# Attention of a conditioned transformer block: lasting PSUM tiles, a split first exp, repeated q and k transfers

## The chip, the cores and the metric

The kernel runs on one core of one Trainium2 chip. The metric is the device time of one execution in microseconds. The kernel before took 3331.09 us (median of 3 runs, 3324.33 to 3333.92).

The core has a matrix engine (TensorE, "PE" in the profile, its weight loads "PEld"), a vector engine (DVE), a scalar engine for functions such as exp (ACT), GpSimd (POOL) and a queue engine (SP) that issues most of the transfers ("SPq"). The engines run their own instruction streams in order and wait for each other by semaphores. TensorE writes its sums to PSUM, which has eight banks of 128 partitions x 512 fp32 values.

## The reference

One block with adaptive layer norm (adaLN) over x of shape 2 x 2048 x 576, with 16 heads of 36 features. The part that matters here is the attention; the rest is cut:

```python
xn = _ln(x, 1e-06)
xn = xn * (1 + sc_msa[:, None, :]) + sh_msa[:, None, :]
qkv = (xn @ w_qkv + b_qkv).reshape(B, N, 3, H, hd)
q, k, v = (qkv[:, :, 0], qkv[:, :, 1], qkv[:, :, 2])
q = _ln(q, 1e-05, qn_g, qn_b)
k = _ln(k, 1e-05, kn_g, kn_b)
attn = jnp.einsum('bqhd,bkhd->bhqk', q, k) * scale
attn = jax.nn.softmax(attn, axis=-1)
o = jnp.einsum('bhqk,bkhd->bqhd', attn, v).reshape(B, N, C)
o = o @ w_proj + b_proj
x = x + g_msa[:, None, :] * o
...
h = jax.nn.gelu(xn2 @ w1 + b1, approximate=False)
m = h @ w2 + b2
x = x + g_mlp[:, None, :] * m
```

Everything is fp32. The kernel has two branches; with these inputs the one called `block_of_small` runs, whose exp needs no maximum.

## The kernel before

**Stages.** For each of the two batches: the qkv projection and head norms (`inputs`), the attention (`attend`), and the output projection (`outputs`). Then the two products of the MLP for both batches. In the trace the attention of the first batch is the stretch from 268 to 1082 us, that of the second from 1396 to 2198 us.

**How q and k lie.** A head has 36 features. 32 of them go to the rows of a "main" tile (`km`, `qm`), one head to each group of 32 partitions, so that four score products run side by side in four row groups. The last four features go to an "ends" tile (`ke`, `qe`) as four parts in 16 rows: each of the four values stands there four times, and `parted` (L767, L768) makes the high or low part of each on DVE with a mask by row (`low_k`, `low_q`). `rows_taken` issues the transfers that fill these tiles out of the projected features (`qo`, `kr`), all on SP's queue: L755 the main rows, L758 the ends, one transfer for each of the four copies. `take_q` does so for one block of 512 queries, `take_k` for all keys of one pair of heads, `take_k_block` for some token tiles of the first pair's keys. Each returns the `parted` work, to be done later.

**The loop of groups.** `attend` goes over 8 head pairs x 4 query blocks x 4 groups, 128 groups in a batch. A group takes four tiles of 128 keys, two at a time (`scores`, L974): each of the four score tiles, called A, B, C, D below in their order, has two halves of 512 queries, one for each head, and each half is a bank of its own. A and B are written together by eight products, then C and D. An exp (L979, ACT) turns a score tile into a `pt` tile in SBUF; there are five `pt` buffers. `values` (L988) then sums the products of v with the four `pt` tiles into the first half of a further PSUM tile, called the sum here. DVE takes the sum out to `ot`: L1034 copies it in the first group of a block, L1036 adds it in the others. TensorE runs one group ahead: its order is scores of group n+1, values of group n, scores of group n+2, and so on. TensorE's and DVE's order in the attention is that of the code; ACT, POOL and SP follow the order that the building layer gives them.

**PSUM.** All PSUM tiles of the attention come from `s_tile`, a pool of four buffers of two banks, which is all of PSUM. A group takes five in turn: A, B, C, D and the sum. So the sum that is made after the scores of a group gets the buffer of that group's A, and the next group's D gets the buffer of that sum. A product into a new tile waits for the last user of the buffer.

**What is put in between.** `later` is a list of work to do some groups later: the masks of `take_q` two groups on, of `take_k` four, the end of a block three (`finish` writes the row sums to DRAM and reads them back over 64 partitions, L1003 and L1004; then `divided` takes the reciprocal, L1007, multiplies, L1008, and issues the stores into `qo`, L1013). `ot` has two buffers, so the copy of L1034 waits for those stores of two blocks ago. `hooks` puts other work into single groups: the transposes of the last two token tiles of q and k (L874, `last_inputs`) in the first four groups, the adaLN products of the first batch in three later ones, and the transfers of the output weights. A hook's own PSUM tile comes from `s_tile` too.

Of the kernel before, what the change touches and what calls it, by code (L numbers as in the profile page):

```python
# [16 lines left out]
P = 128  # L17
# [14 lines left out]
def dit_block(  # L32
# [40 lines left out]

    const = ctx.enter_context(tc.tile_pool(name="const", bufs=1))
    dram = ctx.enter_context(tc.tile_pool(name="dram", bufs=1, space=bass.MemoryType.DRAM))
    psum = {}

    @contextmanager
    def psum_pools():
# [4 lines left out]
            yield  # L84

    def s_tile():
        return psum["s"].tile([P, 2, 512], F32, tag="s", name="s")

    def acc_tile():
# [616 lines left out]
    def block_of_small():  # L706
# [25 lines left out]
        high = kv.tile([P, BLK], F32R, name="high")  # L732

        low_k, low_q, sign_k, sign_q = (kv.tile([P, 1], F32, name=f"part{i}") for i in range(4))
        eights = ident.rearrange("p (r a b) -> p r a b", r=4, a=4)[:, :, 1, :]
        fours = ident.rearrange("p (r a b d) -> p r a b d", r=4, a=4, b=2)[:, :, 0:2, 1, :]
        nc.vector.tensor_reduce(low_k, eights, AX.XY, ALU.add)
        nc.vector.tensor_reduce(low_q, fours, AX.XYZ, ALU.add)
        for low, sign in ((low_k, sign_k), (low_q, sign_q)):
            nc.vector.tensor_scalar(sign, low, -2.0, 1.0, ALU.mult, ALU.add)  # L740
        nc.gpsimd.memset(vv[:, :, :, HD : HD + 1], 1.0)
# [3 lines left out]
        def chunk(c, cols):  # L745
            return qo[:, c, cols] if c < NKC else kr[:, c - NKC, cols]


        def rows_taken(main, ends, halves, first, src, dst):

            for c in halves:
                for h in range(2):
                    r0 = 32 * (2 * c + h)
                    for i, row, d, n in head_rows(first + h * HD, DIMS):
                        nc.sync.dma_start(out=main[r0 + d : r0 + d + n, dst], in_=chunk(i, src(c))[row : row + n, :])  # L755
                    ((i, row, _, n),) = head_rows(first + h * HD + DIMS, HD - DIMS)
                    for j in range(4):
                        nc.sync.dma_start(  # L758
                            out=ends[r0 + n * j : r0 + n * j + n, dst], in_=chunk(i, src(c))[row : row + n, :]
                        )  # L760

        def parted(ends, rows, low, sign):

# [8 lines left out]
        def take_k(p):  # L772
            m, e = km[p % 2], ke[p % 2]
            src = lambda c: slice(c * N // 2, (c + 1) * N // 2)
            rows_taken(m, e, range(2), C + p * 2 * HD, src, slice(0, N // 2))
            return lambda: parted(e, slice(0, P), low_k, sign_k)

        def take_k_block(t0, t1):

            c, k0 = divmod(t0 * P, N // 2)  # L780
            dst = slice(k0, k0 + (t1 - t0) * P)
            rows_taken(km[0], ke[0], (c,), C, lambda c: slice(t0 * P, t1 * P), dst)
            return lambda: parted(ke[0][:, dst], slice(64 * c, 64 * c + 64), low_k, sign_k)

        def take_q(p, qb):
            i = qb % 2
            src = lambda c: slice(qb * BLK, (qb + 1) * BLK)
            rows_taken(qm[i], qe[i], range(2), p * 2 * HD, src, slice(0, BLK))
            return lambda: parted(qe[i], slice(0, P), low_q, sign_q)

        def last_chunk(dst, w, groups, f):
# [162 lines left out]
        def attend(b, pool, hooks):  # L954

            def scores(p, qb, g):  # L960
                i, j = p % 2, qb % 2
                pts = []
                for k0 in (2 * g * P, (2 * g + 1) * P):
                    keys = slice(k0, k0 + P)
                    tiles = [s_tile() for c in range(2)]
                    for k, q, first in (
                        (km[i], qm[j], True),
                        (ke[i].bitcast(F32R), qe[j].bitcast(F32R), False),
                    ):
                        for c in range(2):  # L970
                            for h in range(2):
                                r0 = 32 * (2 * c + h)
                                r = slice(r0, r0 + (DIMS if first else 4 * (HD - DIMS)))
                                nc.tensor.matmul(  # L974
                                    tiles[c][:, h, :], k[r, keys], q[r, :], start=first, stop=not first
                                )
                    for c, ps in enumerate(tiles):
                        pt = pool.tile([P, 2, BLK], F32, name="pt", bufs=5)
                        nc.scalar.activation(pt, ps, AF.Exp, scale=SCALE)  # L979
                        pts.append((pt, k0 // P + c * NT // 2))  # L980
                return pts

            def values(p, pts):
                acc = s_tile()[:, 0, :]
                for pt, kc in pts:
                    for h in range(2):
                        v0 = (kc * H + 2 * p + h) * HV
                        nc.tensor.matmul(  # L988
                            acc[64 * h : 64 * h + 64, :],
                            vt[:, v0 : v0 + 64],  # L990
                            pt[:, h, :],
                            start=pt is pts[0][0],
                            stop=pt is pts[-1][0],
                        )
                return acc

            def finish(p, qb, ot):


                den = pool.tile([P, BLK], F32, name="den")  # L1000
                for h in range(2):
                    sums = den_dram[b, p, qb, h, :]
                    nc.sync.dma_start(out=sums.unsqueeze(0), in_=ot[64 * h + HD : 64 * h + HD + 1, :])  # L1003
                    nc.sync.dma_start(out=den[64 * h : 64 * h + 64, :], in_=sums.partition_broadcast(64))  # L1004

                def divided():
                    nc.vector.reciprocal(den, den)  # L1007
                    nc.vector.tensor_tensor(ot, ot, den, ALU.mult)  # L1008
                    cols = slice(qb * BLK, (qb + 1) * BLK)
                    for h in range(2):  # L1010
                        for c, row, d, n in head_rows((2 * p + h) * HD):
                            for r in (row,) if c < FULL else (row, row + 64):
                                nc.sync.dma_start(  # L1013
                                    out=qo[r : r + n, c, cols], in_=ot[64 * h + d : 64 * h + d + n, :]
                                )

                return divided

            steps = [(p, qb, g) for p in range(NPAIR) for qb in range(NBLK) for g in range(NG)]


            behind, later = None, [[] for _ in range(5)]
            for p, qb, g in [*steps, (None, None, None)]:
                pts = None if p is None else scores(p, qb, g)
                if g == 0 and (p, qb) != (NPAIR - 1, NBLK - 1):
                    later[2].append(take_q(*((p, qb + 1) if qb + 1 < NBLK else (p + 1, 0))))
                if g == 1 and qb == 1 and p + 1 < NPAIR:
                    later[4].append(take_k(p + 1))
                if behind is not None:
                    bp, bqb, bg, bpts = behind  # L1030
                    acc = values(bp, bpts)
                    if bg == 0:
                        ot = pool.tile([P, BLK], F32, name="ot", bufs=2)
                        nc.vector.tensor_copy(ot, acc)  # L1034
                    else:
                        nc.vector.tensor_tensor(ot, acc, ot, ALU.add)  # L1036
                    if bg == NG - 1:
                        later[3].append(finish(bp, bqb, ot))
                if (p, qb, g) in hooks:
                    later[1] += hooks[p, qb, g]() or []  # L1040
                later.append([])
                for do in later.pop(0):
                    do()
                behind = (p, qb, g, pts)
            for do in [do for group in later for do in group]:
                do()
# [80 lines left out]
        for b in range(B):  # L1127
# [30 lines left out]
            def output_opened():  # L1158
# [2 lines left out]
            hooks = {  # L1161
                (0, 0, 0): lambda: last_inputs(NT - 2, range(NKC - 1, NQK)),
                (0, 0, 1): lambda: last_inputs(NT - 1, range(NKC - 1, NQK)),
                (0, 0, 2): lambda: last_inputs(NT - 2, range(NKC - 1)),
                (0, 0, 3): last_inputs_done,
                (4, 0, 1): output_opened,
            }
            if b == 0:
                hooks |= {
                    (0, 2, 1): ada_opened,  # L1170
                    (1, 0, 2): ada_gates,
                    (2, 0, 2): ada_feature_rows,
                    (2, 0, 3): ada_features,
                }
            with tc.manual_schedule(engines={mybir.EngineType.DVE}):
                attend(b, att, hooks)
            close_att()
            wp, close_wp = opening["wp"]
            if b + 1 < B:
# [352 lines left out]
```

## Time and profile before

| What | us |
|---|---|
| Median of 3 runs | 3331.09 |
| The profiled execution's own time | 3329.74 |
| Its span, first to last instruction | 3327.5 |
| TensorE busy | 3250.7 |
| DVE busy | 1457.9 |
| ACT busy | 1440.7 |
| POOL busy | 255.0 |
| TensorE busy in 268.0 to 1082.2 (attention, first batch) | 798.26 of 814.20 |
| ACT busy there | 498.31 |
| TensorE busy in 1390.0 to 2197.6 (attention, second batch) | 794.48 of 807.60 |
| ACT busy there | 503.11 |

The granted clock of TensorE was 0.994 over the span. A line of the page's list of groups names the line of the kernel, the engine, the operation, what is written and read, and the count, then busy time and the mean of one. A line of the timeline begins with the start and the length in us; in brackets stands the idle time of the engine before it and who ended it. A busy TensorE isn't a TensorE at its peak: its instructions overlap, and an instruction that is held at the front of its queue can stand beside one that still runs.

### The profile page before, as it was taken

Reading aid. Unit: us, or ns where it says so; the run is one execution under the profiler, and the core shown is the slowest. Engines: PE = TensorE matmul, PEld = TensorE weight load, DVE = VectorE, ACT = ScalarE, POOL = GpSimd, SP = SyncE. Lnnn points to the kernel's source line nnn. Section 1 sums busy time; section 2 is a strip of 40 time slices with the busy share of each in tenths; the row PEclk is TensorE's granted clock in tenths of the full one; section 3 lists DMA queues with packets and bytes.
Section 4 is the critical chain, followed back from the end, with each engine's and each line's share of the span. In section 5 each row is a group of like instructions: output and inputs, shape, how many; then the busy total and the mean of one; then the engine's idle time right before and its main releaser. Section 6 shows DMA issues by size and latency. Waiting matters only on the chain.

```text
span 3327.5 us, 47009 instructions
## 1 busy us (share of the span) xinstructions
PE 3250.7 (98%) x18143; PEld 1892.2 (57%) x18143; DVE 1457.9 (44%) x2073; ACT 1440.7 (43%) x1928; POOL 255.0 (8%) x249
## 2 busy tenths in 40 slices
PE   8999999999999999999999999998999999999998
PEld 5774333333333777633333333357888788777776
DVE  4664333333333366533333333255455443554554
ACT  2335656666666033356666666633555543000000
POOL 1110000000000211100000000041000000111111
PEclk9999999999999999999999999999999999999999
DMA  3002212212111401021111111144322222523321
GB/s 127 26 27 62 73 44 64 54 45 52 45 44 29 143 26 30 18 57 44 42 42 43 36 44 41 35 169 145 120 84 88 81 81 77 191 100 119 130 100 37
DMA packets 123324, 234.28 MB, mean 70 GB/s; under 512 B 22412, under 2 KB 65365, under 8 KB 121045
## 3 DMA queue, kind: packets, MB, share of 16 engines
q1 hardware_dynamic: 112124, 193.10, 18.8%
q0 software_dynamic: 10240, 36.61, 3.2%
q8 instruction: 146, 2.39, 0.3%
q10 hardware_dynamic: 728, 1.48, 0.1%
q14 instruction: 86, 0.70, 0.1%
HBM read 125.96 MB, written 56.91 MB: 55 GB/s over the span
## 4 chain that ended last, share of the span: by engine, by line
PE 86%; ACT 7%; issue 2%; DMA 2%; DVE 1%; SPq 1%; POOL 0%; ACTq 0%; DVEq 0%; POOLq 0%
PE s L988 28%; PE s L1460 14%; PE s L360 14%; PE s L974 11%; PE m L1310 11%; ACT pt L979 7%; PE m L1324 2%; PE s L371 2%; PE one L1310 2%; PE s L874 1%; DMA wb<-in_w_dram 1%; PE t L1369 1%; SPq L758 0%; PE s L338 0%; DMA qo<-ot 0%
## 5 line engine op out<-in xcount | busy, mean ns | idle before, releaser
L979 ACT ACTIVATE pt<-s 128x1024 f32<-128x1024 f32 x1024 | 994.1, 1024 | 611.2 <-PE s L988 348.0
L988 PE MATMUL s<-pt,vt 128*64 128x512 f32 x4096 | 940.1, 601 | 18.0
L988 PEld LDWEIGHTS s<-pt,vt 128*64 128x64 f32 x4096 | 272.9, 137 | 621.1 <-issue 452.8
L974 PE MATMUL s<-qm,km 32*128 32x512 f32 x4096 | 578.0, 616 | 5.8 <-DVE ot L1034 5.7
L974 PE MATMUL s<-qe,ke 16*128 16x512 f32 x2048 | 430.9, 789 | 5.2 <-DVE ke L768 4.6
L1036 DVE TENSOR_TENSOR ot<-s,ot 128x512 f32<-128x512 f32 x192 | 132.7, 691 | 682.7 <-PE s L988 682.7
L360 PE MATMUL s<-wq,xnt 128*128 128x288 f32 x1536 | 394.2, 412 | 3.6 <-ACT xnt L346 3.6
L974 PEld LDWEIGHTS s<-qm,km 32*128 32x128 f32 x4096 | 193.5, 185 | 280.1 <-ACT pt L979 203.4
L1460 PE MATMUL s<-ws,as 128*128 128x288 f32 x1440 | 351.8, 406 | 0.0
L360 PEld LDWEIGHTS s<-wq,xnt 128*128 128x128 f32 x1536 | 287.1, 191 | 96.0 <-issue 18.5
L1460 PEld LDWEIGHTS s<-ws,as 128*128 128x128 f32 x1440 | 273.6, 190 | 75.6
L1007 DVE RECIPROCAL den<-den 128x512 f32<-128x512 f32 x64 | 213.9, 3343 | 3.8 <-DMA den<-den_dram 3.8
L1310 PE MATMUL m<-xnt,wb 128*128 128x256 f32 x864 | 214.5, 384 | 0.9 <-DVE product L1074 0.9
L1310 PE MATMUL m<-s,wb 128*128 128x256 f32 x864 | 210.2, 379 | 3.1 <-DVE s L1284 3.1
L1034 DVE COPY ot<-s 128x512 f32<-128x512 f32 x64 | 44.2, 691 | 364.6 <-PE s L988 264.3
L974 PEld LDWEIGHTS s<-qe,ke 16*128 16x128 f32 x2048 | 112.0, 185 | 120.6 <-issue 111.9
L1310 PEld LDWEIGHTS m<-s,wb 128*128 128x128 f32 x864 | 164.0, 190 | 26.1 <-DVE s L1284 3.5
L1310 PEld LDWEIGHTS m<-xnt,wb 128*128 128x128 f32 x864 | 159.4, 190 | 33.8 <-issue 12.2
L1337 DVE TENSOR_TENSOR cs<-m,cs 128x512 f32<-128x512 f32 x72 | 49.7, 691 | 233.5 <-ACT cs L1336 157.2
L1460 PE MATMUL s<-ws,hidden 128*128 128x288 f32 x576 | 142.3, 406 | 0.0
L1348 ACT ACTIVATE cs<-cs,b_sb 128x512 f32<-128x512 f32 x144 | 103.9, 722 | 87.4 <-DVE cs L1343 87.4
L1446 DVE TENSOR_TENSOR as<-hidden 128x1152 f32<-128x1152 f32 x80 | 139.5, 1807 | 0.0
(147 smaller groups left out, 2433.2 us busy)
## 6 DMA issues: line engine op xcount, KB each, us to landing
gelu<-cs SPq DMA_DIRECT2D x144, 256.0 KB
hidden<-gelu SPq DMA_DIRECT2D x16, 2304.0 KB
qe<-qo SPq DMA_DIRECT2D x1024, 8.0 KB
den<-den_dram SPq DMA_DIRECT2D x128, 128.0 KB
qm<-qo SPq DMA_DIRECT2D x192, 64.0 KB
xr<-x_dram SPq DMA_DIRECT2D x32, 288.0 KB
out_dram<-y POOLq DMA_DIRECT2D x32, 288.0 KB, 3.7
qo<-ot SPq DMA_DIRECT2D x104, 72.0 KB
```

What stands on the lines that cost most here:

```text
L360: nc.tensor.matmul(outs[a], stationary(k, a), moving(k, a), start=(first and k == 0), stop=(not first and k == FULL - 1),)
L371: nc.tensor.matmul(outs[a], stationary(FULL, a)[r], moving(FULL, a)[r], start=first, stop=not first)
L974: nc.tensor.matmul(tiles[c][:, h, :], k[r, keys], q[r, :], start=first, stop=not first)
L979: nc.scalar.activation(pt, ps, AF.Exp, scale=SCALE)
L988: nc.tensor.matmul(acc[64 * h : 64 * h + 64, :], vt[:, v0 : v0 + 64], pt[:, h, :], start=pt is pts[0][0], stop=pt is pts[-1][0],)
L1007: nc.vector.reciprocal(den, den)
L1036: nc.vector.tensor_tensor(ot, acc, ot, ALU.add)
L1310: nc.tensor.matmul(out_m[m], wb[:, slot[m], k, f * P : (f + 1) * P], moving[m](k), start=k == 0 and (m == 1 or (first and m in (2, 5, 6))) ...
L1324: nc.tensor.matmul(out_m[m], w[r, f * P : (f + 1) * P], a[r, FULL, t * PAIR : (t + 1) * PAIR], start=first and m != 4, stop=not first and ...
L1348: nc.scalar.activation(part, part, AF.Gelu, bias=b1_sb[:, g : g + 1])
L1446: nc.vector.tensor_tensor(stationary[m], x_, y_, op)
L1460: nc.tensor.matmul(ms[m], stationary[m][:, f, :], ws[m][:, f, :], start=(f == 0), stop=(f == HF - 1))
```

## The change

It has five parts, all in the attention.

1. The four PSUM tiles are taken once for a batch's attention and used in turn (`ring`), in place of a new tile from the pool each time.
2. The exp of a group's first tile A is done in two halves, one for each head. The second half is written in the code after the value products of the same step.
3. One transfer with a repeated source fills all 16 rows of a head's ends, in place of four transfers. The four copies of a value now lie next to each other, so the masks `low_k` and `low_q` are made from other columns of the identity.
4. The transfers of `take_k` are issued on GpSimd's queue; those of `take_k_block` and `take_q` stay on SP.
5. The transposes of the last two token tiles' q are two groups later, and the work that a hook returns goes ahead of what is already due in the next group.

```diff
-    psum = {}
+    psum, ring = {}, []
...
     def s_tile():
+        if ring:
+            ring.append(ring.pop(0))
+            return ring[-1]
         return psum["s"].tile([P, 2, 512], F32, tag="s", name="s")
...
-        eights = ident.rearrange("p (r a b) -> p r a b", r=4, a=4)[:, :, 1, :]
-        fours = ident.rearrange("p (r a b d) -> p r a b d", r=4, a=4, b=2)[:, :, 0:2, 1, :]
-        nc.vector.tensor_reduce(low_k, eights, AX.XY, ALU.add)
-        nc.vector.tensor_reduce(low_q, fours, AX.XYZ, ALU.add)
+        parts = ident.rearrange("p (r a b) -> p r a b", a=2, b=2)
+        nc.vector.tensor_reduce(low_k, parts[:, :, 1, :], AX.XY, ALU.add)
+        nc.vector.tensor_reduce(low_q, parts[:, :, :, 1], AX.XY, ALU.add)
...
-        def rows_taken(main, ends, halves, first, src, dst):
+        def rows_taken(queue, main, ends, halves, first, src, dst):
...
-                        nc.sync.dma_start(out=main[r0 + d : r0 + d + n, dst], in_=chunk(i, src(c))[row : row + n, :])
+                        queue.dma_start(out=main[r0 + d : r0 + d + n, dst], in_=chunk(i, src(c))[row : row + n, :])
                     ((i, row, _, n),) = head_rows(first + h * HD + DIMS, HD - DIMS)
-                    for j in range(4):
-                        nc.sync.dma_start(
-                            out=ends[r0 + n * j : r0 + n * j + n, dst], in_=chunk(i, src(c))[row : row + n, :]
-                        )
+                    values = chunk(i, src(c))[row : row + n, :]
+                    queue.dma_start(
+                        out=ends[r0 : r0 + 4 * n, dst],
+                        in_=values.unsqueeze(1).to_broadcast([n, 4, values.shape[1]]),
+                    )
...
-            rows_taken(m, e, range(2), C + p * 2 * HD, src, slice(0, N // 2))
+            rows_taken(nc.gpsimd, m, e, range(2), C + p * 2 * HD, src, slice(0, N // 2))
...
             def scores(p, qb, g):
                 i, j = p % 2, qb % 2
-                pts = []
+                pts, behind = [], []
...
                     for c, ps in enumerate(tiles):
                         pt = pool.tile([P, 2, BLK], F32, name="pt", bufs=5)
-                        nc.scalar.activation(pt, ps, AF.Exp, scale=SCALE)
+                        heads = (slice(0, 2),) if pts else (slice(0, 1), slice(1, 2))
+                        exps = [
+                            lambda pt=pt, ps=ps, h=h: nc.scalar.activation(
+                                pt[:, h, :], ps[:, h, :], AF.Exp, scale=SCALE
+                            )
+                            for h in heads
+                        ]
+                        exps[0]()
+                        behind += exps[1:]
                         pts.append((pt, k0 // P + c * NT // 2))
-                return pts
+                return pts, behind
...
-                pts = None if p is None else scores(p, qb, g)
+                pts, exps = (None, []) if p is None else scores(p, qb, g)
...
                 if behind is not None:
                     bp, bqb, bg, bpts = behind
                     acc = values(bp, bpts)
+                while exps:
+                    exps.pop(0)()
+                if behind is not None:
                     if bg == 0:
...
                 if (p, qb, g) in hooks:
-                    later[1] += hooks[p, qb, g]() or []
+                    later[1] = (hooks[p, qb, g]() or []) + later[1]
...
-                (0, 0, 2): lambda: last_inputs(NT - 2, range(NKC - 1)),
-                (0, 0, 3): last_inputs_done,
+                (0, 1, 0): lambda: last_inputs(NT - 2, range(NKC - 1)),
+                (0, 1, 1): last_inputs_done,
...
+            ring.extend([s_tile() for _ in range(4)])
             with tc.manual_schedule(engines={mybir.EngineType.DVE}):
                 attend(b, att, hooks)
+            ring.clear()
```

More of the change, by code (lines that the diff above doesn't have):

```diff
@@ L781, in take_k_block @@
             dst = slice(k0, k0 + (t1 - t0) * P)
-            rows_taken(km[0], ke[0], (c,), C, lambda c: slice(t0 * P, t1 * P), dst)
+            rows_taken(nc.sync, km[0], ke[0], (c,), C, lambda c: slice(t0 * P, t1 * P), dst)
             return lambda: parted(ke[0][:, dst], slice(64 * c, 64 * c + 64), low_k, sign_k)
@@ L787, in take_q @@
             src = lambda c: slice(qb * BLK, (qb + 1) * BLK)
-            rows_taken(qm[i], qe[i], range(2), p * 2 * HD, src, slice(0, BLK))
+            rows_taken(nc.sync, qm[i], qe[i], range(2), p * 2 * HD, src, slice(0, BLK))
             return lambda: parted(qe[i], slice(0, P), low_q, sign_q)
```

## The prediction

> **What bounds the kernel now.** I read, in this order, the page's busy times and its chain of work that ended last, the busy times by stretch, the timeline of one undisturbed group of the attention, and then every group that lasts longer than its neighbours. From the page:
>
> ```profile
> PE 3250.7 (98%) x18143; PEld 1892.2 (57%) x18143; DVE 1457.9 (44%) x2073; ACT 1440.7 (43%) x1928; POOL 255.0 (8%) x249
> ...
> PE 86%; ACT 7%; issue 2%; DMA 2%; DVE 1%; SPq 1%; POOL 0%; ACTq 0%; DVEq 0%; POOLq 0%
> PE s L988 28%; PE s L1460 14%; PE s L360 14%; PE s L974 11%; PE m L1310 11%; ACT pt L979 7%; PE m L1324 2%; PE s L371 2%; PE one L1310 2%; PE s L874 1%; DMA wb<-in_w_dram 1%; PE t L1369 1%; SPq L758 0%; PE s L338 0%; DMA qo<-ot 0%
> ```
>
> TensorE sets the end; the only other engine with a real share of the chain is ACT, with the exps of L979. Both belong to the attention, the only part that the change touches. One undisturbed group in the timeline (A, B, C, D are the four score tiles of a group, in this order):
>
> ```profile
> 1666.35 3.65 PE L988 MATMUL s<-pt,vt 128*64 128x512 f32 x16
> ...
> 1667.54 2.85 ACT L979 ACTIVATE pt<-s 128x1024 f32<-128x1024 f32 x3 [1.24 <-PE s L988]
> ...
> 1669.94 1.14 PE L974 MATMUL s<-qm,km 32*128 32x512 f32 x8
> 1670.06 0.69 DVE L1036 TENSOR_TENSOR ot<-s,ot 128x512 f32<-128x512 f32 x1 [2.94 <-PE s L988]
> ...
> 1671.13 1.04 PE L974 MATMUL s<-qm,km 32*128 32x512 f32 x8
> 1671.40 1.02 ACT L979 ACTIVATE pt<-s 128x1024 f32<-128x1024 f32 x1 [1.00 <-PE s L974]
> ...
> 1671.59 0.81 PE L974 MATMUL s<-qe,ke 16*128 16x512 f32 x4
> ...
> 1672.47 0.20 PEld L988 LDWEIGHTS s<-pt,vt 128*64 128x64 f32 x4 [0.70 <-ACT pt L979]
> 1672.48 3.65 PE L988 MATMUL s<-pt,vt 128*64 128x512 f32 x16
> ```
>
> All times below count from the start of the value products (here 1666.35). They end at 3.65; the exps of B, C and D run from 1.19 to 4.04 (1667.54 + 2.85 = 1670.39); DVE takes the sum out of PSUM from 3.71 to 4.40; the second pair of score tiles starts at 4.78; the exp of A runs from 5.05 to 6.07, and the next value products start at 6.12 because they write A's buffer, so the full 1.02 us exp must be over. Score products were done 0.08 us sooner (1671.59 + 0.81 = 1672.40). Where the exp is not last, value products start 0.08 us before the end of the score products:
>
> ```profile
> 300.53 0.80 PE L974 MATMUL s<-qe,ke 16*128 16x512 f32 x2
> 301.25 0.20 PEld L988 LDWEIGHTS s<-pt,vt 128*64 128x64 f32 x4 [0.56 <-ACT pt L979]
> ```
>
> So the wait on A's exp costs about 0.15 us in each group. The other view is a group whose eviction is late:
>
> ```profile
> 1733.75 3.65 PE L988 MATMUL s<-pt,vt 128*64 128x512 f32 x16
> ...
> 1738.27 0.69 DVE L1034 COPY ot<-s 128x512 f32<-128x512 f32 x1 [6.24 <-DMA qo<-ot]
> ...
> 1739.01 0.19 PEld L974 LDWEIGHTS s<-qm,km 32*128 32x128 f32 x2 [0.28 <-DVE ot L1034]
> ...
> 1740.30 0.20 PEld L988 LDWEIGHTS s<-pt,vt 128*64 128x64 f32 x4 [0.56 <-ACT pt L979]
> ```
>
> The eviction ends at 1738.96, D's score products wait for it, and the next value products start 1.34 us after its end. In all thirteen groups of the trace that are late for this reason alone it is 1.34 or 1.35. That is a law of this loop: next start = the later of (6.12, end of eviction + 1.34). It decides once the eviction ends after 4.78; today it ends at 4.40, 0.38 us of slack.
>
> How long attention is, from the chain in order of time:
>
> ```profile
> 1075.10 7.09 PE s L988 x32
> ...
> 2190.49 7.09 PE s L988 x32
> ```
>
> The first value products start at 275.59 and 1403.44 (timeline), so 126 intervals take 799.5 and 787.1 us. A regular one is 6.12 to 6.15, say 6.13; 252 of them are 1544.8, and 41.8 us are excess. By the timeline of the long groups: 16.0 at the two starts (transposes of the last q and k, and one wait for ke), 6.5 for the adaLN products, 11.0 behind the adaLN transfers in SP's queue (405 to 457), 8.3 in groups whose eviction waits for a late qo store.
>
> **What the Trainium skill says.** "ScalarE: Activation LUTs", What ACT_TABLE_LOAD costs: 186 ns + 0.833 ns per element with immediate operands, successors overlapping by 93 ns. The trace agrees: 1024 ns for 1024 elements (page, L979; formula 1039), starts 0.92 apart. "PSUM — Partial Sum Buffer", Terms: a tile of two 512-column halves is two banks, and what must not meet is two engines on one bank; an exp of one half beside a product into the other is thus allowed; no run so far shows it. "DMA: Bandwidth & Descriptors", Issuing engines are not separate DMA queues: another issuer saves only issue time. The trace agrees that issue time is the scarce thing: 0.63 us for each 8 KB qe transfer (L758, 2.50 us for four), SP issuing almost without pause around 1500 to 1545.
>
> **The change part by part.** *Ring and half exp.* The listing of the built program shows what waits for what:
>
> ```
> before  DVE  L1036 TensorTensor ot<-s,ot 128x512 [waits PE_49]
> after   ACT  L987 Activation pt<-s 128x512 [waits PE_49]      (A's second half)
> after   DVE  L1053 TensorTensor ot<-s,ot 128x512 [waits Activation_49]
> ```
>
> A's second half stands in ACT's order after B, C and D, and its count of PE_49 is that of the last value product: the sum goes to A's first half, and the dependency is kept for the tile, not the half. The eviction's count of Activation_49 is that of this second half. 254 of 256 groups are built so. The chain after the value products is now:
> - D's exp ends at 4.04, so the second half starts at about 3.94 (0.10 overlap; the value products were over at 3.65). 512 elements: 1.024 - 512 x 0.833 ns = 0.60 us, to 4.54.
> - Eviction: hand-over 0.04, start 4.58, 0.69 us, end 5.27.
> - D's products wait; next value products at 5.27 + 1.34 = 6.61.
>
> What is removed: value products would start at about 5.97 if A's first half (5.05 + 0.60 = 5.65) were the only matter. The 0.15 gain is not reached, because D's tile, not A's exp, is late. Behind the eviction on DVE stand the reciprocal (3.34) and product (0.69) of a block: 5.27 + 4.03 = 9.30, that is 2.69 in the next group, before its eviction is due. ACT has 4.2 of 6.6 us of work. Cost: (6.61 - 6.13) x 252 = +121 us. In the last group of a batch there are no scores between, and its value products need the second half at 4.54 rather than follow at 3.43: +1.1 twice, +2.
>
> *One transfer for four parts.* On SP 16 qe issues of a block become 4: 768 fewer x 0.63 = 480 us less queue time. Issue time doesn't grow with rows: a 64-row read with repeats (den, L1004) takes 0.58. Landing is hidden by two groups. The qo stores then come in time: the 8.3 us go, and of the 11.0 I keep 2. *k on GpSimd.* About nine issues for each of 14 pairs at 0.54 us (POOL's own in the trace) are 5 us, landed some 4 us later, while the masks wait four groups (24 us) on: hidden by POOL's idleness in this stretch. Uncovered, DVE would stand in order before the eviction. *Last q two groups later.* Each set of transposes keeps its cost; now DVE does their four or five copies (0.34 each) after the late eviction, and D's tile is theirs, so such a group takes about 5.27 + 1.4 + 1.34 = 8.0 (8.3 for five). The ke wait of the third group (2.94 us in the waits) shrinks to about 1, as fewer issues and no transposes stand before it and the hooks' masks now go ahead of the other deferred work. Starts: (1.7 + 2 x 1.4 + 1.0) x 2 = 11 for 16. adaLN products: 5.5 for 6.5, a part falling into D's wait. Excess after: 11 + 5.5 + 2 = 18.5 for 41.8, -23. The mask reductions at the start are one-off, under 0.1.
>
> Sum: +121 + 2 - 23 = +100 on the profiled execution's own 3329.7 (span 3327.5): 3429.7; the median of the runs is 1.4 above that execution. I forecast 3430.
>
> Bounds: the second half's start between 3.70 (at once after the value products, if D's exp were earlier) and 4.05 (no overlap): a group of 6.37 to 6.72; the excess between 10 and 35.
>
> **Rivals.**
> - *The second half runs straight after the value products.* 6.37: +0.24 x 252 = 60, +2 - 23: 3369. For it: its own wait is over at 3.65. Against: ACT keeps its order and D is before it in every built group.
> - *Faster: the eviction isn't held.* If it ended before 4.78, which needs the second half over by 4.06, values would start at 5.97: -0.16 x 252 = -40, -23: 3267. For it: ACT has a hole of 1.24 us ahead of B's exp, into which the half would fit. Against: the built order puts it after D.
> - *GpSimd's queue is late.* If a pair's k landed after its masks are due, DVE stops in order before an eviction: 5 us each x 14 on top, 3500. Against: 24 us of cover for 9.
>
> **How the numbers follow.** Forecast 0.82, first rival 0.08, faster 0.05, GpSimd late 0.05. Their own range is 6.50 to 6.72 per group with the excess bounds, 3395 to 3465; I add the room down towards the first rival: 3385 to 3465. A difference under 0.3% (10 us) can't be told from none: within it 0.02, slower 0.93, faster 0.05.
>
> **What would show it.** Right: DVE's eviction (L1051, L1053) put down to ACT pt, starting about 4.6 after the value products; PEld L979 waiting for DVE ot in nearly all groups; groups of about 6.6; no DVE wait on qo stores. Wrong: the eviction still released by PE at 3.7, or value products 5.97 apart, or DVE waiting for DMA ke.

## The result, and the profile after

The changed kernel took 3423.95 us (median of 4 runs, 3419.96 to 3425.91), the kernel before 3327.86 us on the same chip (3324.33 to 3333.92; one run more than the three of the table above). The ratio is 1.0285, with a 95% interval from 1.0265 to 1.0306: the change made the kernel slower by 2.7 to 3.1%. The forecast of 3430 is 6 us above the median and inside its range.

| What | Before, us | After, us |
|---|---|---|
| The profiled execution's own time | 3329.74 | 3424.05 |
| Its span | 3327.5 | 3422.3 |
| First value products of the two batches | 275.59 and 1403.44 | 272.62 and 1444.22 |
| 252 intervals between value products, sum | 1586.6 | 1680.0 |
| A regular interval | 6.13 | 6.60 |

The intervals alone are 93.4 us longer, and the own time 94.3. So the loss lies in the loop of groups. The last value products of each batch add 1.14 us (8.23 for 7.09), and the rest of the kernel is 1.4 us shorter. The page of the changed kernel, busy times and the chain that ended last:

```profile
PE 3374.3 (99%) x18143; PEld 1948.9 (57%) x18143; DVE 1458.1 (43%) x2073; ACT 1455.4 (43%) x2184; POOL 317.5 (9%) x369
...
PE 94%; DVE 1%; DMA 1%; issue 1%; ACT 1%; POOL 0%; SPq 0%; ACTq 0%; POOLq 0%; DVEq 0%
PE s L1002 26%; PE s L979 22%; PE s L365 13%; PE s L1479 13%; PE m L1329 11%; PE m L1343 2%; PE s L376 2%; PE one L1329 2%; ACT pt L987 1%; PE s L879 1%; DMA wb<-in_w_dram 1%; PE t L1388 1%; PE s L343 0%; DMA gb_rows<-rows_dram 0%; DVE xt L273 0%
```

These lines mislead if they are read alone. TensorE has the same 18143 matmuls, yet its busy time is 124 us longer and stands at 99%. ACT's share of the chain fell to 1%, though ACT now stands in the way of every group. The reason is in the score products (before, then after):

```profile
L974 PE MATMUL s<-qm,km 32*128 32x512 f32 x4096 | 578.0, 616 | 5.8 <-DVE ot L1034 5.7
...
L979 PE MATMUL s<-qm,km 32*128 32x512 f32 x4096 | 720.1, 626 | 1.8 <-DVE qo L888 1.2
```

One product takes nearly as long as before (626 ns for 616), but their busy time grew by 142 us, because fewer of them run side by side: before, the products of C and D started together; now C's run alone for 0.5 us until D's may start. A moment counts as busy when any product runs. So one needs the view by group (the changed kernel's timeline):

```profile
1700.71 3.65 PE L1002 MATMUL s<-pt,vt 128*64 128x512 f32 x16
...
1701.89 3.35 ACT L987 ACTIVATE pt<-s 128x1024 f32<-128x1024 f32 x4 [2.21 <-PE s L1002]
...
1705.27 0.69 DVE L1053 TENSOR_TENSOR ot<-s,ot 128x512 f32<-128x512 f32 x1 [4.73 <-ACT pt L987]
1705.49 1.22 PE L979 MATMUL s<-qm,km 32*128 32x512 f32 x6
1705.72 0.60 ACT L987 ACTIVATE pt<-s 128x512 f32<-128x512 f32 x1 [0.48 <-PE s L979]
...
1706.02 0.19 PEld L979 LDWEIGHTS s<-qm,km 32*128 32x128 f32 x2 [0.33 <-DVE ot L1053]
...
1707.30 0.20 PEld L1002 LDWEIGHTS s<-pt,vt 128*64 128x64 f32 x4 [0.56 <-issue]
```

The value products end at 1700.71 + 3.65 = 1704.36. ACT runs four exps in one piece: B, C, D and, as the fourth, the second half of A, to 1701.89 + 3.35 = 1705.24. The eviction starts 0.03 us later, at 4.56 in the group's own time, and was 3.71 before. It ends at 5.25; D's score products wait for it; the next value products start at 6.60, which is 5.25 + 1.35. In the kernel before, the eviction was over when D's products were due, and A's exp came last. The releasers of the changed kernel (engine, line, releaser; then us in total, times, longest) show that this is so in nearly every group:

```profile
DVE ot L1053 <- ACT pt L987: 776.6, 190, 6.2
...
DVE ot L1051 <- ACT pt L987: 364.7, 62, 5.9
...
PEld s L979 <- DVE ot L1053: 62.0, 184, 0.6
...
DVE ot L1051 <- DMA den<-den_dram: 11.8, 2, 5.9
```

252 evictions are released by ACT (before, 237 were released by TensorE's L988), and D's weight load waits for DVE. The 776.6 us are idle time of an engine that has little to do, and no measure of the damage; the damage is 0.85 us of delay per eviction, of which 0.38 were slack and 0.47 remain. The waits on `qo` stores (81.9 us in 12 groups before) are gone. Two waits are put down to the row sums read back from DRAM; they stand in groups of the usual 6.60 us, so they cost nothing.

### The profile page after: what moved, and what is told of

It is laid out like the page before. It is cut to its first block, busy times and chain, and to the rows that moved or that the text cites. A ratio compares the mean times of both kernels' runs of the same rounds, so it can differ in the third digit from the quotient of the medians.

```text
span 3422.3 us, 45158 instructions
## 1 busy us (share of the span) xinstructions
PE 3374.3 (99%) x18143; PEld 1948.9 (57%) x18143; DVE 1458.1 (43%) x2073; ACT 1455.4 (43%) x2184; POOL 317.5 (9%) x369
## 4 chain that ended last, share of the span: by engine, by line
PE 94%; DVE 1%; DMA 1%; issue 1%; ACT 1%; POOL 0%; SPq 0%; ACTq 0%; POOLq 0%; DVEq 0%
PE s L1002 26%; PE s L979 22%; PE s L365 13%; PE s L1479 13%; PE m L1329 11%; PE m L1343 2%; PE s L376 2%; PE one L1329 2%; ACT pt L987 1%; PE s L879 1%; DMA wb<-in_w_dram 1%; PE t L1388 1%; PE s L343 0%; DMA gb_rows<-rows_dram 0%; DVE xt L273 0%
## 5 line engine op out<-in xcount | busy, mean ns | idle before, releaser
L987 ACT ACTIVATE pt<-s 128x1024 f32<-128x1024 f32 (+1 forms) x1280 | 1008.9, 858 | 692.2 <-PE s L1002 563.7
L979 PE MATMUL s<-qm,km 32*128 32x512 f32 x4096 | 720.1, 626 | 1.8 <-DVE qo L888 1.2
L979 PE MATMUL s<-qe,ke 16*128 16x512 f32 x2048 | 550.9, 768 | 0.7 <-DVE ke L773 0.7
L1053 DVE TENSOR_TENSOR ot<-s,ot 128x512 f32<-128x512 f32 x192 | 132.8, 691 | 776.6 <-ACT pt L987 776.6
L979 PEld LDWEIGHTS s<-qm,km 32*128 32x128 f32 x4096 | 255.0, 184 | 359.1 <-ACT pt L987 252.7
L365 PEld LDWEIGHTS s<-wq,xnt 128*128 128x128 f32 x1536 | 286.4, 191 | 93.3 <-issue 18.5
L979 PEld LDWEIGHTS s<-qe,ke 16*128 16x128 f32 x2048 | 149.1, 184 | 119.2 <-issue 116.4
```

The source lines that it names most:

```text
L365: nc.tensor.matmul(outs[a], stationary(k, a), moving(k, a), start=(first and k == 0), stop=(not first and k == FULL - 1),)
L979: nc.tensor.matmul(tiles[c][:, h, :], k[r, keys], q[r, :], start=first, stop=not first)
L987: lambda pt=pt, ps=ps, h=h: nc.scalar.activation(pt[:, h, :], ps[:, h, :], AF.Exp, scale=SCALE)
```

## The experiments

Every kernel was measured beside the kernel before on its own chip. The first four and the last one tell apart where the loss comes from, the other four what the rest of the change is worth.

| Run | Edit | Median, us | Kernel before there | Ratio, 95% interval | Regular group, us |
|---|---|---|---|---|---|
| after | | 3423.95 | 3327.86 | 1.0285 [1.0265, 1.0306] | 6.60 |
| e1_whole | exp of A whole | 3299.97 | 3330.55 | 0.9908 [0.9892, 0.9925] | 6.12 |
| e2_early | A in halves, both at once | 3315.90 | 3330.55 | 0.9958 [0.9944, 0.9972] | 6.19 |
| e3_split_only | before + ring + late half | 3437.08 | 3330.55 | 1.0322 [1.0301, 1.0344] | 6.60 |
| e4_banks | eight one-bank tiles, all exps in halves | 3265.57 | 3330.55 | 0.9809 [0.9793, 0.9825] | 5.98 |
| e5_pool | e1 without the ring | 3301.52 | 3329.09 | 0.9920 [0.9906, 0.9934] | as e1 |
| e6_k_on_sp | e1, k on SP's queue | 3301.72 | 3329.09 | 0.9917 [0.9903, 0.9931] | as e1 |
| e7_q_early | e1, last q and hooks' work in the old places | 3306.21 | 3329.09 | 0.9933 [0.9919, 0.9947] | as e1 |
| e8_four | e1, four transfers per head's ends | 3322.43 | 3329.09 | 0.9980 [0.9974, 0.9987] | as e1, late ones again |
| e9_late | e1, one more copy ahead of each eviction | 3371.66 | 3330.33 | 1.0123 [1.0106, 1.0140] | 6.39 |

### The split exp alone: whole, early, and without the other parts

e1_whole keeps the rest of the change and makes the exp of A in one piece again:

```diff
-                        heads = (slice(0, 2),) if pts else (slice(0, 1), slice(1, 2))
+                        heads = (slice(0, 2),)
```

> The changed kernel with A's exp in one piece again; ring, transfers and the moved q stay. Theory (the wait is the eviction behind A's second half): evictions start 3.71 after the value products and are released by PE, groups last 6.13 instead of 6.60, so 3424 - 0.47 x 252 - 2 = 3303, under the kernel before by its removed excess of about 25. Rival (GpSimd's queue or the ring itself costs something): stays above 3330.

It took 3299.97 us, 124 us less than the changed kernel (126 by the two ratios) and 0.75 to 1.08% less than the kernel before. So the split exp is the whole loss, and the other four parts are a gain of some 30 us.

e2_early keeps the two halves, but issues the second straight after the first:

```diff
-                        exps[0]()
-                        behind += exps[1:]
+                        for exp in exps:
+                            exp()
```

> The changed kernel with A's second half issued right after its first half, ahead of the value products; everything is still computed. Theory: the value products again wait for both halves, 5.05 + 0.51 + 0.60 + 0.05 = 6.2, the eviction is over at 4.40: groups of 6.20, 3424 - 0.40 x 252 - 2 = 3321. Rival (the price is ACT's own: one more exp of 0.2 us fixed cost and its semaphore in each group, wherever it stands): groups stay near 6.6, 3424.

Its timeline:

```profile
1639.53 0.69 DVE L1053 TENSOR_TENSOR ot<-s,ot 128x512 f32<-128x512 f32 x1 [1.54 <-PE s L1002]
...
1640.80 1.08 ACT L987 ACTIVATE pt<-s 128x512 f32<-128x512 f32 x2 [1.00 <-PE s L979]
...
1641.94 1.51 PE L1002 MATMUL s<-pt,vt 128*64 128x512 f32 x6
```

Those value products follow a piece that began at 1635.76. The eviction is back at 3.77 and released by TensorE. The next value products start at 6.18, 0.06 after the end of both halves (1640.80 + 1.08 = 1641.88). The first half alone was over some 0.5 us sooner. The score products ended at about 1641.00 + 0.81 = 1641.81, so that without a wait the value products would have started at 1641.73, by the 0.08 us that the prediction read. They don't start there, although they write only the first half of A's tile. So splitting as such costs 0.06 us a group (two exps of 512 take 1.08 where one of 1024 takes 1.02), and 3315.9 - 3300.0 = 16 us in all; the other 108 of the 124 us come from the place of the second half. The same view also says why the split could bring nothing here: the product waits for the tile, not for the half.

e3_split_only puts only the ring and the late half into the kernel before:

> The kernel before with the ring and the split exp alone; transfers and the last q as before. Theory: groups of 6.6 as in the changed kernel, the transfers' excess partly kept: 3328 + 0.47 x 252 + 2 - a few (late evictions partly fall into the new wait) = 3440 to 3448. Rival (transfers or GpSimd carry a part of the loss): clearly below 3424.

3437.08 us, just under the expected range, and regular groups of 6.60: the split makes its loss without the other parts. The surplus over regular groups was 28.1 us, and not the 41.8 of the kernel before. Outside the stretch of the adaLN transfers the groups with late `qo` stores are regular here, although the transfers are those of the kernel before. Two things are in the trace. An eviction that a store held up a little falls into a wait that is there anyway. And the stores themselves come earlier: in the second batch's groups 21, 37 and 101 the last store was issued 3.2, 2.2 and 3.5 us after the start of the value products in the kernel before; here it is 0.6 us after it, in the group before, and 0.2 us after it. That fits SP's having 6.60 us for what it had to issue in 6.13. The parts of a change thus don't simply add up: beside the split the other parts are worth some 13 us (3437.08 - 3423.95), without it some 30.

### A tile for each bank

e4_banks makes eight lasting tiles of one bank each, in place of four of two, and all exps in halves, issued in order. A pair of tiles stands where one tile stood:

```diff
-            ring.extend([s_tile() for _ in range(4)])
+            close_psum()
+            close_psum = opened_psum(h=8)
+            banks = [psum["h"].tile([P, 512], F32, tag="h", name="h") for _ in range(8)]
+            ring.extend([Banks(banks[2 * i : 2 * i + 2]) for i in range(4)])
...
+                        for h in range(2):
+                            nc.scalar.activation(pt[:, h, :], ps[:, h, :], AF.Exp, scale=SCALE)
```

> The changed kernel with eight lasting tiles of one bank each in place of four of two, and all exps in halves (eight of 512 per group): the sum now has a tile of its own after A's first half is read, so neither the value products nor the eviction wait for A's second half. Theory: value products wait for 5.65 at most and start at 5.97, eviction over at 4.40, exps of B to D over at 4.32 before their tiles are due at 4.78: groups of 5.97, 3424 - 0.63 x 252 - 3 = 3262, under both kernels. Rival (more exps cost time by themselves): four more exps of 0.2 us each, slower than 3424.

It took 3265.57 us, 1.8 to 2.1% less than the kernel before, 34 us less than e1_whole and 158 less than the changed kernel. A group of it in the timeline:

```profile
1641.85 3.65 PE L1002 MATMUL h<-pt,vt 128*64 128x512 f32 x16
1643.04 3.05 ACT L993 ACTIVATE pt<-h 128x512 f32<-128x512 f32 x6 [1.04 <-PE h L1002]
...
1645.61 0.69 DVE L1053 TENSOR_TENSOR ot<-h,ot 128x512 f32<-128x512 f32 x1 [5.29 <-ACT pt L993]
...
1646.89 1.09 ACT L993 ACTIVATE pt<-h 128x512 f32<-128x512 f32 x2 [0.81 <-PE h L987]
...
1647.83 3.65 PE L1002 MATMUL h<-pt,vt 128*64 128x512 f32 x16
```

and the chain that ended last, in order of time (start, length, what):

```profile
1639.53 2.40 PE h L987 x23
1641.92 3.58 PE h L1002 x16
1645.51 2.40 PE h L987 x23
1647.90 3.58 PE h L1002 x16
```

The value products start at 1647.83, before the exps of A are over (1646.89 + 1.09 = 1647.98), so they don't wait for its second half. The eviction starts at 3.76, as in e1. The bracket names ACT, but the only exps of that bank are those of A in the piece before, over since about 1642.0 (1641.85 + 0.15); what came last is TensorE's last product, at 1641.85 + 3.65 = 1645.50. In this stretch the chain knows no other engine any more. Regular groups are 5.98 us, where the prediction worked out 5.97 for a group that nothing but TensorE holds up. This is the gain that the split was able to give, with a tile for each bank. One-bank tiles with the second half still late were not run.

### The law of the late eviction

e9_late delays the eviction in e1 by DVE alone: one extra copy of the sum, into a scratch tile, stands ahead of it.

```diff
+                    nc.vector.tensor_copy(high.bitcast(F32), acc)
```

> Ring and whole exp (3300), with one more copy of the sum into a scratch tile ahead of each eviction, so that the eviction ends 0.61 later, at 5.01 instead of 4.40 after the value products, while no exp and no ACT wait changes. Theory (the next value products start 1.34 after the eviction's end once that is later than 4.78): groups of 6.35 in place of 6.13, 3300 + 0.22 x 252 = 3355. Rival (in the changed kernel the loss came through ACT, and 0.38 us of slack or more hides DVE): 3300.

```profile
1704.91 3.65 PE L1002 MATMUL s<-pt,vt 128*64 128x512 f32 x16
...
1708.67 0.69 DVE L1049 COPY high<-s 128x512 f32<-128x512 f32 x1 [5.10 <-PE s L1002]
...
1709.27 0.68 DVE L1052 COPY ot<-s 128x512 f32<-128x512 f32 x1
...
1711.30 1.08 PE L1002 MATMUL s<-pt,vt 128*64 128x512 f32 x4
```

The eviction ends at 1709.27 + 0.68 = 1709.95, or 5.04, and the next value products start at 6.39, 1.35 later. The constant 1.34 to 1.35 thus holds in three ways of being late: a store (before), ACT (after), DVE (here). The time came out 17 us over the expectation. Regular groups of 6.39 for the 6.35 expected are 10 us of that, because the copy starts at 3.76 and not at 3.71, as the eviction of e1 does too; of the rest, about 4 lie in the groups with transposes (0.5 to 0.6 longer than in e1, where the others are 0.27 longer) and in four groups of 6.75. The other 3 were not followed.

### What the other parts are worth

These four are e1 with one more part undone. e5_pool takes the lasting tiles away:

```diff
-            ring.extend([s_tile() for _ in range(4)])
```

> A's exp whole and PSUM tiles from the pool as in the kernel before; the transfers, the order of the hooks and the moved q as in the changed kernel. Theory: with the exp whole the ring is worth nothing, since the same products wait for the same exps: 3300, within 5 of the version with ring and whole exp. Rival (the ring saves waits on TensorE's and ACT's queues that were on the path): 10 or more above it.

3301.52 us, and its runs overlap with those of e1: no effect of the ring can be told here. e6_k_on_sp puts the transfers of k back:

```diff
-            rows_taken(nc.gpsimd, m, e, range(2), C + p * 2 * HD, src, slice(0, N // 2))
+            rows_taken(nc.sync, m, e, range(2), C + p * 2 * HD, src, slice(0, N // 2))
```

> Ring and whole exp (3300), but k's transfers on SP again, one for each four parts. Theory: SP then has about nine issues more in one of four blocks, 6 us of a block of 24.5, and room for them: 3300 to 3303. Rival (GpSimd's queue is what freed the evictions): some evictions wait for qo stores again, 3305 or more.

3301.72 us: 2 us by the medians, 3 by the ratios, not told apart from nothing. e7_q_early undoes the fifth part:

```diff
-                    later[1] = (hooks[p, qb, g]() or []) + later[1]
+                    later[1] += hooks[p, qb, g]() or []
...
-                (0, 1, 0): lambda: last_inputs(NT - 2, range(NKC - 1)),
-                (0, 1, 1): last_inputs_done,
+                (0, 0, 2): lambda: last_inputs(NT - 2, range(NKC - 1)),
+                (0, 0, 3): last_inputs_done,
```

> Ring and whole exp (3300), but the last q's transposes again in the third and fourth group, and the hooks' work behind what is already due. Theory: the wait for ke in the third group comes back in part at both starts: 3301 to 3308. Rival (moving q was worth nothing): 3300.

3306.21 us, 6 more than e1. In both batches the third group's scores wait for the last masks of ke again, up to 3.0 us in place of 0.5, and these intervals take 9.4 and 10.7 us in place of 7.1 and 7.0. In the second batch the clock fell too (last section). e8_four takes the single repeated transfer away, with the masks that go with it:

```diff
-                    queue.dma_start(
-                        out=ends[r0 : r0 + 4 * n, dst],
-                        in_=values.unsqueeze(1).to_broadcast([n, 4, values.shape[1]]),
-                    )
+                    for j in range(4):
+                        queue.dma_start(out=ends[r0 + n * j : r0 + n * j + n, dst], in_=values)
```

> Ring and whole exp (3300), but four transfers for each head's ends again, those of k on GpSimd, those of q on SP. Theory (issue time on SP made the excess): q's 16 more issues in each block nearly fill SP where finish's transfers and adaLN's stand in it: 3308 to 3320. Rival (GpSimd's part alone freed SP enough): 3300 to 3304.

3322.43 us, 22 more than e1 and slightly over the expected range. Among its waits the stores are back, and ke is late:

```profile
DVE ot L1050 <- DMA qo<-ot: 13.3, 2, 7.4
...
DVE high L771 <- DMA ke<-kr: 8.9, 4, 2.9
```

The interval with the wait for ke takes 11.3 us in both batches (7.1 and 7.0 in e1), which is 8.5 us, and about once for each pair of heads a group takes 6.3 to 6.5. In all the 252 intervals are 16 us longer than e1's. The other 6 of the 22 lie outside the loop, 4 of them after the last value products, where the traces of all the runs differ by up to 8 us. So the one transfer is worth 16 to 22 of the 30 us, and not for its bytes, since the bytes written are the same. At the start it is the issuing: SP needs 7.7 us for the transfers of the first pair's last keys (279.6 to 287.3), in e1 3.6 (278.5 to 282.1). Elsewhere it may also be the packets, 128806 for 122796; that was not told apart.

## Why the prediction was right

**The split exp and its wait.** This was the step that decided, and it held term by term:

| Term | Worked out | Measured |
|---|---|---|
| Second half, length | 0.60 | 0.60 |
| Eviction, start to end | 4.58 to 5.27 | 4.56 to 5.25 |
| End of eviction to next value products | 1.34 | 1.35 |
| Group | 6.61 | 6.60 |
| Last value products of a batch, each | +1.1 | +1.14 |
| The split and its waits in all | +123 | +124 beside the other parts (after against e1_whole), +107 alone (e3) |

The price of an element of exp held too: the two forms stand in the changed kernel's groups as

```profile
L987 ACT ACTIVATE pt<-s 128x1024 f32<-128x1024 f32 x768 | 731.2, 1025 | 563.7 <-PE s L1002 563.7
...
L987 ACT ACTIVATE pt<-s 128x512 f32<-128x512 f32 x512 | 311.0, 607 | 128.5 <-PE s L979 128.5
```

1025 - 607 = 418 ns for 512 elements, or 0.82 each, where the prediction took 0.833. The 0.02 us by which the eviction is sooner are 0.01 in the end of the exps (4.53 for 4.54) and 0.01 in the hand-over (0.03 for 0.04).

**The surplus over regular groups.** Forecast 18.5 us, 16.8 by the sum of the intervals (1680.0 - 252 x 6.60). The starts took 10.9 (11 forecast): groups with transposes took 7.9 or 8.3 us (8.0 and 8.3), the wait for ke added 1.1 in each batch (1.0). The adaLN groups took 5.0 (5.5), and the queue behind them nothing (2). The stores' 8.3 went, as forecast, but not for the reason alone that was given: they went in e3 as well, without the new transfers. The 16.0 at the starts before held a cost that the prediction didn't name: after the two waits for ke the clock was at half, and the value products took 4.92 and 5.43 us for 3.65, which is 3.05 us in all. Two groups of 6.9 in the second batch are left, whose exps began 0.3 us late; their cause wasn't followed.

**k on GpSimd, the ring, the order of q.** Forecast at nothing, nothing and a few us within the surplus; e6, e5 and e7 show 2, 2 and 6, the first two not told apart from nothing. The prediction put the repeated transfer and the moved q at -23 beside the split. The surplus fell by 25.0 (41.8 to 16.8), but e3 shows that 13.7 of it (41.8 to 28.1) come with the split itself, whose longer groups take up the late stores. The size was right, the attribution only for about half of it; that the rest fell away by the split was luck.

**The rest of the 6 us.** 252 x 0.01 for the group (2.5) and 1.7 for the surplus are 4.2; 1.4 lie outside the loop, and the rest is rounding. One sum of the prediction is off without consequence: its own terms (6.72 a group, an excess of 35) give an upper end of 3475, not 3465.

**The rivals.** The second half straight after the value products is excluded by the unbroken series of four on ACT. That the eviction isn't held is excluded by the 252 waits. GpSimd's queue being late is excluded: no DVE wait on `ke` or `km` transfers of k is in the trace, and e6 changes nothing. What wasn't tried is a second half placed before D in ACT's order: its gain remains worked out, not shown.

The Trainium skill, "PSUM — Partial Sum Buffer", Terms, names two engines on one bank as what must not meet. e4's 5.98 us agrees that a bank's exp may run while a product writes the other. In the changed kernel the building layer nevertheless kept the order for the whole tile of two banks; e2's 6.19 beside e4's 5.98 shows it from the other side. The kernel opens its PSUM pools with `reuse_waits="tile"`; whether that setting has a part in it was not tried.

## What to carry to other kernels

When an instruction is moved later in the code, look for what it stands behind on its own engine, and for who waits for its tile: here 0.60 us of exp, moved behind the last exp, held up the eviction, which held up the next products, and 0.47 us went 252 times over. A split of work over the halves of a tile pays only if what waits also waits by halves; give each bank a tile of its own before splitting, and read in the waits that the second user really starts at the end of its half. A busy share of 99% doesn't exclude a wait, since one product is enough to make a moment busy; so compare the length of one loop step, not the busy share.

## What the runs showed of the hardware

**Issue time, not bytes.** Issuing four 8 KB transfers of `qe` took SP's queue 2.50 us (before, at 1659.58), and four of 32 KB 2.90 (after, at 1702.43): four times the bytes for 0.10 us more each. Four in place of one cost 22 us over the kernel (e8). The Trainium skill, "DMA: Bandwidth & Descriptors", Issuing engines are not separate DMA queues, says that another issuer saves only the time of issuing; e6 agrees (moving k to another issuer shows nothing, once the count is down), but the count itself mattered.

**A wait of about 3 us slowed TensorE for longer than it lasted.** In e7's third group of the second batch TensorE's weight loads waited 2.96 us for ke. Its busy times by stretch (length, then busy time and instructions of PE, PEld, DVE, ACT and POOL, granted clock, share and rate of DMA) are:

```profile
1397.00:1400.70 3.70, 1.52 (x11) 0.66 (x10) 3.54 (x9) 1.02 (x1) 0.00 (x0) 0.92 0.02 4
1400.70:1403.50 2.80, 2.79 (x14) 1.52 (x14) 0.00 (x0) 0.00 (x0) 0.00 (x0) 0.50 0.00 0
1403.50:1409.00 5.50, 5.50 (x20) 1.64 (x19) 0.02 (x1) 2.77 (x3) 0.00 (x0) 0.69 0.30 64
1412.28:1418.40 6.12, 6.09 (x42) 2.25 (x40) 0.69 (x1) 3.88 (x4) 0.00 (x0) 1.00 0.78 264
```

After the wait the clock was 0.50, and the value products took 5.29 us in place of 3.65. The Trainium skill, "TensorE: Matmul & The Clock Gate", Part 1, describes this: an idle window of about 3.4 us brings half the clock, and a busy one the full clock back. Here shorter waits were enough, and not only once: in the kernel before the waits for ke of 2.94 and 2.91 us were followed by value products of 4.92 and 5.43. The length of the wait alone doesn't decide it: 2.64 us in e3 (a late store) were followed by 5.35, and 2.75 in the first batch of e7 left the products at 3.65. With 1.2 us in the changed kernel and 0.5 in e1 no value products took longer than 3.66, which is part of what the moved q is worth.
